# A state-space recurrence put into source order on three engines, with part of the next stages' work set between its groups

## The chip, the cores and the metric

The kernel runs on one core of one Trainium2 chip. The metric is the device time of one launch in microseconds (us). The kernel before takes 2572.84 us, the median of three runs (2568.23 to 2574.86). Everything else about time in this document is read from one profiled execution.

## The reference

The input is `x` (512 tokens x 512 channels) and a context of 8192 x 512. Three blocks follow each other, all in f32, and each adds its result to its input:

```python
x = x + cross_attention(layernorm(x), ctx)       # 16 heads of 64, 8192 keys
u = layernorm(x)
x = x + mamba_and_mlp(u)
x = x + experts(layernorm(x))

def mamba_and_mlp(u):
    h = rmsnorm(u) * norm1_w
    xin, z = split(h @ in_proj.T)                 # 1024 channels each
    xin = silu(causal_conv4(xin) + conv_b)
    dt, B, C = split(xin @ x_proj.T)              # 32, 16, 16
    delta = softplus(dt @ dt_proj.T + dt_b)
    # per channel c and state n, over the tokens t, one after the other:
    #   H[t] = exp(delta[t]*A[c,n]) * H[t-1] + delta[t]*xin[t]*B[t,n]
    #   y[t] = sum_n H[t]*C[t,n]
    y = (y + xin * D) * silu(z)
    u = u + y @ out_proj.T
    h = rmsnorm(u) * norm2_w
    return u + (silu(h @ w1.T) * (h @ w3.T)) @ w2.T       # w1, w3: 512 -> 2048

def experts(v):
    # top 2 of 16 experts by v @ router.T, gate sigmoid(logit), 512 -> 512 -> 512 (SwiGLU)
    return gated_sum_of_two_experts(v) + shared_swiglu(v)   # shared: 512 -> 1024 -> 512
```

The recurrence has 1024 channels x 16 states x 512 tokens. It is sequential over the tokens only.

## The kernel before

The first part, the cross-attention, isn't touched. It ends at about 1868 us of the span. All that follows is in `tail`. There the 512 tokens are worked in two halves of 256 (`s` = 0, 1; `H` = 256). Products of weights use f16 pairs (a high and a low part, three matmuls), and their results are scaled by `IW` on the way out of PSUM.

**The steps of a half, by name.**
- `wo_proj(s)` (L1067) is the attention's output projection. It adds to `x_sb`, two 128-token rows at a time.
- `prep(s)` (L774) makes the two norms (`stats`, `rsqrt`), the scaled `h`, its transposes `hT`, the input projection `pxz`, the convolution (on TensorE by diagonal matrices `dg` for half 1), the silu pair `xin` and `xs` (`silu_split`), and the product `psd` that gives dt, B and C. B and C go to DRAM (`bc_d`) and come back broadcast to all 128 partitions by `load_bc(s, k)` (L866), four loads of 128 x 1024 for each of B (k = 0) and C (k = 1), issued on SP.
- `delta(s, q)` (L876) makes delta and `du` (delta times xin) for 256 channels (`q`, two blocks `b` of 128), with five activations on ScalarE and four VectorE steps, then the product `pz` and its silu `zs`. `lnexp` reloads the activation table after each Silu.
- `scan(s, b)` (L906) is the recurrence of one 128-channel block, in four groups of four states. A group has: four exponentials `dA` on ScalarE (L916); in half 1 a copy of the carried state `carry` into column 0 of `hs` (L918); the multiply of B by `du` (L919); the scan itself over 128 x 1028 (L923); in half 0 the copy of the last state out to `carry` (L925); the multiply by C in place (L926); and four identity matmuls that sum the states into the PSUM tile `py` (L929). A block ends with the term of D (L930). There are 64 groups. `dAs` and `hss` hold three buffers each.
- `gate(s, q, yT)` (L932) multiplies `py` by `zs` and splits the product into an f16 pair `yT`.
- `outproj(s, yT, h2)` (L939) is the output projection, the rmsnorm of its sum (`rsqrt` with the tag c) and the transposes into `h2`.
- The MLP of a half has eight blocks of 256 hidden channels. Each block loads three weight tiles, forms `pg` and `pu`, takes `g = silu(pg) * pu`, splits it into the pair `gg` (a ScalarE copy, then a VectorE subtraction), and adds a down product into two accumulators. `ffn` (L963) states the steps plainly; `ffn_ordered` (L989) holds the down product of a block back until the next block's `pg` and `pu` are issued. The shared experts use the same function with four blocks (`RS`).
- `ln2(s, xT)` (L1034) is the last norm (`rsqrt` with the tag d), its transposes and the router's logits `lg`.
- `route()` (L1171) forms the two chosen experts of each token, one-hot rows `oh`, the rank of each token in its expert's list by the matmul `prk`, from it the slot `sg` and the gate `gs`, and scatters all tokens' rows (`xf`) twice into `xd_d` in DRAM by indirect DMAs on POOL's queue. The experts (`moe_load`, `moe_in` and so on) load 128 rows of `xd_d` each; the first of these loads stand on POOL's queue too, behind the scatters.
- `early()` loads, converts and splits one of the first 20 pieces of the experts' weights (`wef` to `we`).

**Shared buffers.** All weight tiles of the projections and the MLP come by `wload` (L766) on SP's queue into five buffers `wpm`, so a load starts when the buffer's last reader is done. `bank_j` gives three PSUM banks in turn for all short products; `acc` gives the longer accumulators.

**What sets the order.** In the recurrence the program states the steps block by block and the Tile scheduler orders the instructions of all engines by its own priorities: a loop over the eight pairs (s, q) calls `scan(s, 2*q)`, one step of `prep(1)` or of the MLP `ffn(0)`, the gate of the pair before, `delta` of the pair after, and `scan(s, 2*q + 1)`. Of the MLP of half 0 seven of the eight blocks are stated there. From `outproj(1)` on TensorE, VectorE and ScalarE keep the source's order (`tc.manual_schedule`); SP and POOL stay with the scheduler. The stages behind it are driven by generators: `ffn_ordered(1)` with `ln2(0)` at its steps 0, 5, 7 and 9, then the four shared blocks of half 0 with `ln2(1)` and the head of `route`, then the four of half 1 with the rest of `route`, then the experts.

The code of both parts follows.

Of the kernel before, what the change touches and what calls it, by code (L numbers as in the profile page):

```python
# [17 lines left out]
P = 128  # L18
# [18 lines left out]
XR = 2 * DM + 4  # L37
NWE = 20
# [601 lines left out]
def tail(tc, a, out, const, scr, ident, x_sb, mlp_d, oT, sum_d, xd_d, psums):  # L640
# [133 lines left out]
    def prep(s):  # L774
# [4 lines left out]
        nc.vector.tensor_scalar(v1, mv[:, :, 1], 1e-5, None, ALU.add)  # L779
        rsqrt(r1, v1, 2, f"a{s}")  # L780
        nc.vector.tensor_mul(v2, r1, r1)
        nc.vector.tensor_mul(v2, v2, mv[:, :, 1])
        nc.vector.tensor_scalar(v2, v2, 1e-6, None, ALU.add)
        rsqrt(r2, v2, 2, f"b{s}")
        nc.vector.tensor_mul(r2, r2, r1)
# [10 lines left out]
        hT[s] = hp  # L796
        transposeT(h, hp[:, 0], hp[:, 1], scale=nw[:, 0])
# [12 lines left out]
        for i in range(4):  # L810
# [4 lines left out]
            xp = m2.tile([P, 2, H + 3], F32, name="xp", bufs=2)  # L815
            nc.scalar.activation(xp[:, :, 3:], ps, AF.Copy, scale=IW)
# [3 lines left out]
            if s:  # L820
                pc = bank_j([P, 2, H], F32, "pc")
                for j in range(2):
                    e = 2 * i + j
                    dg = m2.tile([P, 4, P], F32, name="dg", tag="w2k", bufs=5)
                    for q in range(4):
                        nc.scalar.activation(dg[:, q], ident, AF.Copy, scale=cw[:, e, q : q + 1])
                    for q in range(4):
                        nc.tensor.matmul(
                            pc[:, j, :], lhsT=dg[:, q], rhs=xp[:, j, q : q + H], start=q == 0, stop=q == 3
                        )  # L830
                silu_split(s, i, pc)
# [20 lines left out]
        for i in range(8):  # L852
            nc.tensor.matmul(psd, lhsT=xpw[:, 0, i], rhs=xs[:, 0, i], start=i == 0, stop=False)
            nc.tensor.matmul(psd, lhsT=xpw[:, 0, i], rhs=xs[:, 1, i], start=False, stop=False)
            nc.tensor.matmul(psd, lhsT=xpw[:, 1, i], rhs=xs[:, 0, i], start=False, stop=i == 7)
        xd = m2.tile([64, H], F32, name="xd", tag="w2k", bufs=5)
# [6 lines left out]
        load_bc(s, 0, m1)  # L863
# [12 lines left out]
    def delta(s, q):  # L876
# [6 lines left out]
        rl = w2("rl")  # L883
        nc.scalar.activation(ex, pd, AF.Abs, scale=IW)
# [3 lines left out]
        nc.scalar.activation(lg, u1, AF.Ln)  # L888
        nc.vector.scalar_tensor_tensor(ex, u1, -1.0, ex, ALU.add, ALU.subtract)
# [7 lines left out]
        for j in range(2):  # L897
            mm_block(pz[:, j, :], wz, j, hT[s][:, 0], hT[s][:, 1])
        zs = m2.tile([P, 2, H], F32, name="zs", bufs=2)
        nc.scalar.activation(zs, pz, AF.Silu, scale=IW)  # L900
        lnexp()
        dlu[s, q] = [dl, du, zs]

    turn = [0]

    def scan(s, b):  # L906
        q, j = b // 2, b % 2
        if j == 0:
            dlu[s, q].append(ps_s.tile([P, 2, H], F32, name="py", tag="pss"))
        dl, du, zs, py = dlu[s, q]  # L910
        for nq in range(4):
            dA, hs = dAs[turn[0] % 3], hss[turn[0] % 3]
            turn[0] += 1
            for n in range(4):
                k = nq * 4 + n
                nc.scalar.activation(dA[:, n, 1:], dl[:, j], AF.Exp, scale=Av[:, b, k : k + 1])  # L916
            if s:
                nc.scalar.copy(hs[:, :, 0], carry[:, b, nq * 4 : nq * 4 + 4])  # L918
            nc.vector.tensor_tensor(  # L919
                hs[:, :, 1:], BC[s][0, nq], du[:, j].unsqueeze(1).to_broadcast((P, 4, H)), ALU.mult  # L920
            )
            hf = hs.rearrange("p n t -> p (n t)")
            nc.vector.tensor_tensor_scan(hf, dA.rearrange("p n t -> p (n t)"), hf, 0.0, ALU.mult, ALU.add)  # L923
            if s == 0:
                nc.scalar.copy(carry[:, b, nq * 4 : nq * 4 + 4], hs[:, :, H])  # L925
            nc.vector.tensor_mul(hs[:, :, 1:], hs[:, :, 1:], BC[s][1, nq])  # L926
            for n in range(4):
                k = nq * 4 + n
                nc.tensor.matmul(py[:, j, :], lhsT=ident, rhs=hs[:, n, 1:], start=k == 0, stop=False)  # L929
        nc.tensor.matmul(py[:, j, :], lhsT=dD[:, b], rhs=xin[s][:, b, :], start=False, stop=True)  # L930

    def gate(s, q, yT):  # L932
        dl, du, zs, py = dlu.pop((s, q))
        y = m2.tile([P, 2, H], F32, name="y", tag="w2k", bufs=5)
        nc.vector.tensor_mul(y, py, zs)
        nc.scalar.copy(yT[:, 0, 2 * q : 2 * q + 2, :], y)
        nc.vector.tensor_tensor(yT[:, 1, 2 * q : 2 * q + 2, :], y, yT[:, 0, 2 * q : 2 * q + 2, :], ALU.subtract)

    def outproj(s, yT, h2, fill=None):  # L939
        wout = [wload("outp", i) for i in range(4)]  # L940
        for i in range(2):
            px = bank_j([P, DM], F32, "px")
            for k in range(8):
                sl = slice(i * P, (i + 1) * P)
                mm_down(px, yT[:, 0, k, sl], yT[:, 1, k, sl], wout[k // 2], k % 2, k == 0, k == 7)
            nc.vector.scalar_tensor_tensor(u_sb[:, 2 * s + i], px, IW, u_sb[:, 2 * s + i], ALU.mult, ALU.add)
        ts_ = slice(2 * s, 2 * s + 2)
# [4 lines left out]
        nc.vector.tensor_scalar(ms, ms, 1e-6, None, ALU.add)  # L952
        rsqrt(rr, ms, 2, f"c{s}")
        h = F.tile([P, 2, DM], F32, name="h", tag="h", bufs=1)
        for i in range(2):
            nc.vector.tensor_scalar(h[:, i], u_sb[:, 2 * s + i], rr[:, i : i + 1], None, ALU.mult)
        if not s:
            nc.vector.tensor_add(x_sb[:, ts_, :], x_sb[:, ts_, :], u_sb[:, ts_, :])
        if fill:
            fill()  # L960
        transposeT(h, h2[:, 0], h2[:, 1], scale=nw[:, 1])

    def ffn(s, h2, names, pm):  # L963
        nf = len(mlp_d[names[0]])
        for f2 in range(nf):
            wg, wu, wd = (wload(n, f2) for n in names)
            pg = bank_j([P, 2, H], F32, "pg")
            pu = bank_j([P, 2, H], F32, "pu")
            for j in range(2):
                mm_block(pg[:, j, :], wg, j, h2[:, 0], h2[:, 1])  # L970
            for j in range(2):
                mm_block(pu[:, j, :], wu, j, h2[:, 0], h2[:, 1])
            g = F2.tile([P, 2, H], F32, name="g32", bufs=2)
            nc.scalar.activation(g, pg, AF.Silu, scale=IW)
            nc.vector.scalar_tensor_tensor(g, pu, IW, g, ALU.mult, ALU.mult)
            gg = F2.tile([P, 2, 2, H], F16, name="gg", bufs=2)
            nc.scalar.copy(gg[:, 0], g)
            nc.vector.tensor_tensor(gg[:, 1], g, gg[:, 0], ALU.subtract)
            yield
            for i in range(2):  # L980
                sl = slice(i * P, (i + 1) * P)
                for j in range(2):
                    k = 2 * f2 + j
                    mm_down(pm[i], gg[:, 0, j, sl], gg[:, 1, j, sl], wd, j, k == 0, k == 2 * nf - 1)
        for i in range(2):
            nc.vector.scalar_tensor_tensor(x_sb[:, 2 * s + i], pm[i], IW, x_sb[:, 2 * s + i], ALU.mult, ALU.add)
# [508 lines left out]
```

## Time and profile before

| what | value |
|---|---|
| median of three runs | 2572.84 us (2568.23 to 2574.86) |
| profiled execution, its own time | 2565.43 us |
| its span on the core | 2563.7 us |
| mean granted TensorE clock | 0.979 of full speed |
| TensorE (PE) busy | 2361.3 us, 92% of the span |
| VectorE (DVE) busy | 2046.2 us, 80% |
| ScalarE (ACT) busy | 1947.5 us, 76% |
| GpSimd (POOL) busy | 73.8 us, 3% |
| moved by DMA | 529.52 MB, 207 GB/s |

The shares are means over stages with different limits, and three quarters of the span are the attention, which the change does not touch. So they say little about the change: it has to be read from the stages behind 1868 us, each by itself. In the profile PE is a matmul, PEld the load of its stationary operand, which runs beside it; SP only issues DMAs. An entry such as `hs<-bc,du` names what is written and what is read, `x64` how often, and a bracket or a last column names the engine, operation and line that ended a wait. L919 is line 919 of the kernel. A stage between two cuts `A:B` is given with its length and with the busy time of each engine in it.

### The profile page before, as it was taken

To read this page: it belongs to the slowest core of one execution; us is meant where nothing else is said; L and a number is where in the kernel's file an instruction comes from. 1 tells how busy PE (TensorE), PEld (TensorE's weight loads), DVE (VectorE), ACT (ScalarE), POOL (GpSimd) and SP (SyncE) were. 2 spreads that over 40 slices of the span, in tenths; PEclk is the share of its full clock that TensorE was granted. 3 is DMA by queue.
4 is the path that set the end of the run, shared out by engine and by line. 5 is a ranking of instruction groups with operands and counts; after the bars stand their busy time and mean duration, and the time that the engine had idled before them with its cause. 6 is when DMAs were issued, how large, how long until landed. Compare 5 with 4: busy or idle time off the path is not lost. (4 is left out here: it accounts for less than half of the span.)

```text
span 2563.7 us, 56681 instructions
## 1 busy us (share of the span) xinstructions
PE 2361.3 (92%) x22958; PEld 1722.3 (67%) x22958; DVE 2046.2 (80%) x2378; ACT 1947.5 (76%) x3734; POOL 73.8 (3%) x77
## 2 busy tenths in 40 slices
PE   7999899999999999999999998998878678899896
PEld 3555577777666777766777776897756456577775
DVE  6776578888888888887888777998899999746685
ACT  5787788888878888877888888997958557434685
POOL 3000000000000000000000000000000000001112
PEclk9999999999999999999999999999999889999998
DMA  7983777787777787777778664777711212388897
GB/s 267 304 272 133 215 213 227 231 238 232 216 231 227 219 247 236 226 213 213 240 216 234 175 171 133 196 207 210 200 59 40 101 50 84 125 281 274 315 360 232
DMA packets 355199, 529.52 MB, mean 207 GB/s; under 512 B 28194, under 2 KB 221922, under 8 KB 354660
## 3 DMA queue, kind: packets, MB, share of 16 engines
q1 hardware_dynamic: 349156, 513.23, 65.7%
q0 software_dynamic: 3616, 8.66, 1.5%
q8 instruction: 182, 2.98, 0.5%
q10 hardware_dynamic: 2160, 3.95, 0.5%
q14 instruction: 85, 0.70, 0.1%
HBM read 396.65 MB, written 126.97 MB: 204 GB/s over the span
## 5 line engine op out<-in xcount | busy, mean ns | idle before, releaser
L380 DVE TENSOR_TENSOR phl<-p,phl 128x1024 f16<-128x1024 f32 x512 | 626.8, 1225 | 191.5 <-ACT phl L377 175.6
L375 ACT ACTIVATE p<-pss 128x512 f32<-128x512 f32 x1024 | 597.6, 622 | 112.1 <-issue 43.5
L308 ACT ACTIVATE sf<-psx 128x512 f16<-128x512 f32 x1024 | 558.6, 625 | 70.2 <-PE psx L303 69.5
L367 PE MATMUL pss<-qhh,k 128*128 128x256 f16 x2048 | 478.3, 274 | 14.1 <-ACT phl L377 11.9
L368 PE MATMUL pss<-qlm,kb 128*128 128x256 f16 x2048 | 477.1, 273 | 0.8 <-DMA v<-v_d 0.7
L316 DVE TENSOR_TENSOR runm<-runm,sf 128x2048 f16<-128x2048 f16 x240 | 292.4, 1220 | 51.4 <-ACT sf L308 51.3
L397 PE MATMUL po<-v,phl 128*128 128x130 f16 x4096 | 322.3, 220 | 3.9 <-DVE oq L410 3.4
L377 ACT ACTIVATE phl<-pss 128x512 f16<-128x512 f32 x512 | 312.8, 611 | 0.0
L397 PEld LDWEIGHTS <-phl 128*128 128x128 f16 x4096 | 270.5, 98 | 61.7 <-issue 15.3
L278 PE MATMUL psv<-wh_v,ctxc 128*128 128x256 f16 x1024 | 283.4, 277 | 7.3 <-ACT wh_v L179 3.2
L279 PE MATMUL psv<-wl_v,ctxc 128*128 128x256 f16 x1024 | 282.0, 275 | 1.1 <-DVE wl_v L180 1.1
L280 PE MATMUL psv<-wh_v,ctxc 128*128 128x256 f16 x1024 | 282.0, 275 | 0.0
L367 PEld LDWEIGHTS <-k 128*128 128x128 f16 x2048 | 200.3, 98 | 65.0 <-issue 20.0
L368 PEld LDWEIGHTS <-kb 128*128 128x128 f16 x2048 | 200.7, 98 | 52.1 <-issue 14.9
L303 PE MATMUL psx<-khl,qh 64*128 64x512 f16 x1024 | 208.1, 386 | 18.2 <-ACT sf L308 13.1
L929 PE MATMUL py<-hs,ident 128*128 128x256 f32 x512 | 141.2, 430 | 76.6 <-DVE hs L926 76.5
L400 PE MATMUL po<-v,phl 128*128 128x65 f16 x4096 | 208.2, 193 | 1.4 <-DVE phl L380 1.4
L254 PE MATMUL psk<-ctxc,wh_k 128*128 128x512 f16 x512 | 197.4, 386 | 10.8 <-ACT ctxc L237 9.0
L379 DVE CAST phl<-p 128x1024 f16<-128x1024 f32 x256 | 176.1, 688 | 30.8 <-ACT p L375 30.6
L255 PE MATMUL psk<-ctxc,wh_k 128*128 128x512 f16 x512 | 196.0, 383 | 0.9 <-DVE ctxc L238 0.9
L256 PE MATMUL psk<-ctxc,wl_k 128*128 128x512 f16 x512 | 195.9, 383 | 0.0
L929 PEld LDWEIGHTS py<-hs,ident 128*128 128x128 f32 x512 | 104.8, 213 | 108.3 <-DVE hs L926 90.9
(315 smaller groups left out, 3814.4 us busy)
## 6 DMA issues: line engine op xcount, KB each, us to landing
v<-v_d SPq DMA_DIRECT2D x128, 520.0 KB
k<-k_d SPq DMA_DIRECT2D x256, 256.0 KB
ctxc<-ctx_d SPq DMA_DIRECT2D x96, 512.0 KB
wef<-in_gu_dram SPq DMA_DIRECT2D x72, 512.0 KB
v_d<-vs SPq DMA_DIRECT2D x128, 260.0 KB
k_d<-khl SPq DMA_DIRECT2D x128, 256.0 KB
kb<-k_d SPq DMA_DIRECT2D x128, 256.0 KB
wpm<-w_d SPq DMA_DIRECT2D x48, 512.0 KB
```

What stands on the lines that cost most here:

```text
L278: nc.tensor.matmul(ps[:, t, :], lhsT=ct[i // 2][:, 0, i % 2, sl], rhs=wh[:, i, :], start=i == 0, stop=False)
L279: nc.tensor.matmul(ps[:, t, :], lhsT=ct[i // 2][:, 0, i % 2, sl], rhs=wl[:, i, :], start=False, stop=False)
L280: nc.tensor.matmul(ps[:, t, :], lhsT=ct[i // 2][:, 1, i % 2, sl], rhs=wh[:, i, :], start=False, stop=i == NC4 - 1)
L308: nc.scalar.activation(dst, ps, AF.Copy, scale=1.0 / (8.0 * WS))
L316: nc.vector.tensor_tensor(r, r, sf, ALU.max)
L367: nc.tensor.matmul(ps[:, hh], lhsT=k[:, hh, sl], rhs=qhh[:, hh, qs], start=True, stop=False)
L368: nc.tensor.matmul(ps[:, hh], lhsT=b[:, hh, sl], rhs=qlm[:, hh, qs], start=False, stop=True)
L375: nc.scalar.activation(p32[:, i], pss[i], AF.Exp, scale=sc)
L377: nc.scalar.activation(ph[:, i], pss[i], AF.Exp, scale=sc)
L380: nc.vector.tensor_tensor(pl, p32, ph, ALU.subtract)
L397: nc.tensor.matmul(o, lhsT=ph[:, i, hh, qs], rhs=vv, start=first, stop=False, **kw)
L929: nc.tensor.matmul(py[:, j, :], lhsT=ident, rhs=hs[:, n, 1:], start=k == 0, stop=False)
```

## The change

The loop over (s, q) and `scan` are replaced by a loop over the 64 groups, one slot per group, and the manual order now opens ahead of this loop: TensorE, VectorE and ScalarE keep the source's order through the recurrence too. In slot g stand, in this order: the carries, the exponentials of group g+1, the multiply and the scan of group g, the multiply by C of group g-1, and the sums of group g-2; then, in fixed slots of each eight, the two steps of a gate and four steps of a `delta`; then side work. The side work of half 0 (slots 0 to 31) is `wo_proj(1)` and `prep(1)`. That of half 1 (slots 36 to 63) is `outproj(0)`, the whole MLP of half 0, its `ln2` and two of the four blocks of its shared experts. `PACE` says how many of its steps a slot takes (1.3 and 1.4). The generators have more `yield` marks, so that the two ends of a hand-off between engines can lie in two slots. `ffn` is gone; `ffn_ordered` can do a range of blocks. The broadcast loads of B and C for half 1 stand at slots 31 and 32. Behind the recurrence, `ffn_ordered(1)` runs without `ln2(0)`, half 0 has two shared blocks left, and `ln2(1)` stands at their steps 3, 5 and 7, with `route` from step 8 on.

```diff
+PACE = (1.3, 1.4)
...
@@ prep(s): more marks, only for half 1
         nc.vector.tensor_scalar(v1, mv[:, :, 1], 1e-5, None, ALU.add)
+        if s:
+            yield
         rsqrt(r1, v1, 2, f"a{s}")
+        if s:
+            yield
...
+                yield
+                pc = bank_j([P, 2, H], F32, "pc")
...
+                yield
                 silu_split(s, i, pc)
...
-        load_bc(s, 0, m1)
+        if not s:
+            load_bc(s, 0, m1)
...
@@ delta(s, q)
         rl = w2("rl")
+        yield
         nc.scalar.activation(ex, pd, AF.Abs, scale=IW)
...
         nc.scalar.activation(lg, u1, AF.Ln)
+        yield
         nc.vector.scalar_tensor_tensor(ex, u1, -1.0, ex, ALU.add, ALU.subtract)
...
+        dlu[s, q] = [dl, du]
+        yield
         zs = m2.tile([P, 2, H], F32, name="zs", bufs=2)
         nc.scalar.activation(zs, pz, AF.Silu, scale=IW)
         lnexp()
-        dlu[s, q] = [dl, du, zs]
-    turn = [0]
-    def scan(s, b):
...
+        dlu[s, q].append(zs)
+        yield
+    def exps(g):
+        s, b, nq = groups[g]
+        dA = dAs[g % 3]
+        for n in range(4):
+            k = nq * 4 + n
+            nc.scalar.activation(dA[:, n, 1:], dlu[s, b // 2][0][:, b % 2], AF.Exp, scale=Av[:, b, k : k + 1])
+    def states(g):
...
+        nc.vector.tensor_tensor(
+            hs[:, :, 1:], BC[s][0, nq], du[:, b % 2].unsqueeze(1).to_broadcast((P, 4, H)), ALU.mult
+        )
+        hf = hs.rearrange("p n t -> p (n t)")
+        nc.vector.tensor_tensor_scan(hf, dA.rearrange("p n t -> p (n t)"), hf, 0.0, ALU.mult, ALU.add)
+    def carry_in(g):
...
+            nc.scalar.copy(hss[g % 3][:, :, 0], carry[:, b, nq * 4 : nq * 4 + 4])
+    def carry_out(g):
...
+            nc.scalar.copy(carry[:, b, nq * 4 : nq * 4 + 4], hss[g % 3][:, :, H])
+    def outputs(g):
...
+        nc.vector.tensor_mul(hs[:, :, 1:], hs[:, :, 1:], BC[s][1, nq])
+    def sums(g):
...
+        for n in range(4):
+            nc.tensor.matmul(py[:, j, :], lhsT=ident, rhs=hs[:, n, 1:], start=nq + n == 0, stop=False)
+        if nq == 3:
+            nc.tensor.matmul(py[:, j, :], lhsT=dD[:, b], rhs=xin[s][:, b, :], start=False, stop=True)
...
@@ outproj(s, yT, h2)
                 mm_down(px, yT[:, 0, k, sl], yT[:, 1, k, sl], wout[k // 2], k % 2, k == 0, k == 7)
+                if k % 4 == 3:
+                    yield
...
+        yield
         rsqrt(rr, ms, 2, f"c{s}")
+        yield
...
-        if not s:
-            nc.vector.tensor_add(x_sb[:, ts_, :], x_sb[:, ts_, :], u_sb[:, ts_, :])
-        if fill:
-            fill()
+        nc.vector.tensor_add(x_sb[:, ts_, :], x_sb[:, ts_, :], u_sb[:, ts_, :])
+        yield
         transposeT(h, h2[:, 0], h2[:, 1], scale=nw[:, 1])
-    def ffn(s, h2, names, pm):
...
-    def ffn_ordered(s, h2, names, pm):
+    def ffn_ordered(s, h2, names, pm, lo=0, hi=None):
...
-        for f2 in range(nf):
+        for f2 in range(lo, hi or nf):
...
@@ the recurrence; taken out is the loop over (s, q) with scan, gate, delta, outproj(0) and ffn(0)
+    groups = [(s, b, nq) for s in range(2) for b in range(8) for nq in range(4)]
+    def side0():
+        yield from wo_proj(1)
+        xin[1] = const.tile([P, 2, 8, H], F32, name="xin1", tag="big16")[:, 0]
+        yield from prep(1)
+    def side1():
+        yield from outproj(0, yTs[0], h2s[0])
+        yield from ffn_ordered(0, h2s[0], MLP, [acc(3), acc(3)])
+        xT0 = h2tile()
+        yield from ln2(0, xT0)
+        rs0.extend([xT0, [acc(3), acc(3)]])
+        yield from ffn_ordered(0, xT0, RS, rs0[1], 0, 2)
...
+    exps(0)
+    for g in range(64):
+        s, b, nq = groups[g]
+        i, r = g // 8, g % 8
+        carry_in(g)
+        if g:
+            carry_out(g - 1)
+        if g + 1 < 64:
+            exps(g + 1)
+        states(g)
+        if g:
+            outputs(g - 1)
+        if g == 31:
+            for _ in sides[0]:
+                pass
+            load_bc(1, 0, m1)
+        if g == 32:
+            load_bc(1, 1, m3)
+        if g > 1:
+            sums(g - 2)
+        if r == 2 and i:
+            gt_ = gate(*seq[i - 1], yTs[-1])
+            next(gt_)
+        if r == 3 and i:
+            next(gt_)
...
+            dl_ = delta(*seq[i + 1])
+        if r in (3, 4, 5, 6) and i < 7:
+            next(dl_)
+        if s == 0 or g > 35:
+            due += PACE[s]
+            while given < due:
+                given += 1
+                next(sides[s], None)
+    outputs(63)
+    sums(62)
+    sums(63)
...
+    for n, _ in enumerate(outproj(1, yTs[-1], h2s[1])):
+        if n >= 4:
+            next(sides[1], None)
+    for _ in sides[1]:
         pass
...
@@ behind the recurrence
-    xT0, xT1 = h2tile(), None
-    l0 = ln2(0, xT0)
     for n, _ in enumerate(mlp1):
-        if n in (0, 5, 7, 9):
-            next(l0, None)
         if n % 3 == 1:
             early()
...
-    for n, _ in enumerate(rs0):
-        if n in (4, 5, 7):
+    for _ in ffn_ordered(0, rs0[0], RS, rs0[1], 2, 4):
+        n += 1
+        if n in (3, 5, 7):
             next(l1, None)
         elif n > 7:
             next(ro, None)
         if n % 3 == 1:
             early()
+    for _ in l1:
+        pass
```

## The prediction, made before the changed kernel ran

> **What bounds the kernel now.** I read the stage table first (busy time of each engine between cuts that I set at the first `hs` multiply, at the end of the last `hs*C` multiply, at the start of the second half's MLP, at its end, at the start of half 1's shared experts and at the start of the experts).
>
> ```profile
> core 0: us, PE busy (x) PEld busy (x) DVE busy (x) ACT busy (x) POOL busy (x), PEclk, DMA share, GB/s
> 1868.32:2217.66 349.34, 264.85 (x1385) 198.15 (x1384) 337.04 (x299) 222.88 (x498) 4.68 (x5) 0.92 0.21 68
> 2217.66:2246.60 28.94, 28.19 (x173) 17.85 (x172) 10.38 (x24) 8.79 (x14) 0.14 (x1) 1.00 0.62 213
> 2246.60:2312.61 66.01, 64.62 (x513) 48.30 (x512) 28.35 (x43) 24.85 (x35) 0.00 (x0) 1.00 0.81 276
> 2312.61:2347.40 34.79, 33.72 (x287) 25.14 (x286) 21.85 (x46) 17.87 (x24) 0.00 (x0) 1.00 0.77 266
> 2347.40:2381.06 33.66, 31.48 (x246) 23.39 (x243) 20.80 (x43) 11.63 (x15) 12.92 (x14) 1.00 0.89 316
> 2381.06:2563.70 182.64, 155.16 (x2088) 127.11 (x2088) 125.74 (x123) 131.04 (x159) 33.12 (x18) 0.95 0.88 298
> ```
>
> The reader is to see that two stages have different owners. In the recurrence (349.3 us) VectorE works 337.0 us and idles 12.3: it is the bound. In the next four rows TensorE works 158.0 of 163.4 us. The change takes TensorE work out of these rows and puts it into the first, where TensorE has room, but with it VectorE work, where VectorE has none. Then the groups of VectorE in the recurrence, and its order of time:
>
> ```profile
> L923 DVE TENSOR_TENSOR_SCAN hs<-dA,hs 128x1028 f32<-128x1028 f32 x64 | 145.3, 2291 | 2.6 <-ACT dA L916 2.5
> L926 DVE TENSOR_TENSOR hs<-hs,bc 128x1024 f32<-128x1024 f32 x64 | 76.9, 1216 | 1.1 <-ACT carry L925 1.1
> L919 DVE TENSOR_TENSOR hs<-bc,du 128x1024 f32<-128x1024 f32 x64 | 76.0, 1216 | 0.7 <-PE py L929 0.6
> ```
>
> ```profile
> 1937.72 1.20 DVE L919 TENSOR_TENSOR hs<-bc,du 128x1024 f32<-128x1024 f32 x1
> 1938.84 1.22 DVE L926 TENSOR_TENSOR hs<-hs,bc 128x1024 f32<-128x1024 f32 x1
> 1939.97 2.29 DVE L923 TENSOR_TENSOR_SCAN hs<-dA,hs 128x1028 f32<-128x1028 f32 x1
> ...
> 1946.64 1.20 DVE L919 TENSOR_TENSOR hs<-bc,du 128x1024 f32<-128x1024 f32 x1
> 1947.88 2.30 DVE L923 TENSOR_TENSOR_SCAN hs<-dA,hs 128x1028 f32<-128x1028 f32 x1
> ```
>
> From start to start a multiply takes 1.12 to 1.13 us when the next instruction is another group's (1937.72 to 1938.84), 1.24 when the next is its own scan (1946.64 to 1947.88). The groups lose only 4.4 us to others: the scheduler has put other work into every wait. What an unfilled wait costs shows after the recurrence, where the order is already that of the source:
>
> ```profile
> 2239.09 0.16 DVE L672 TENSOR_TENSOR nw_c<-rr 128x2 f32<-128x2 f32 x1 [1.78 <-ACT rr L670]
> ...
> 2257.28 0.69 DVE L1015 SCALAR_TENSOR_TENSOR g<-pu,g 128x512 f32<-128x512 f32 x1
> 2258.65 0.69 DVE L1018 TENSOR_TENSOR gg<-g,gg 128x512 f16<-128x512 f32 x1 [0.68 <-ACT gg L1017]
> ```
>
> Last, what TensorE waits for at the start of the experts, and POOL's order of time there:
>
> ```profile
> PE pxd L1315 <- DMA xd<-xd_d: 2.2, 1, 2.2
> ```
>
> ```profile
> 2351.84 1.11 POOL L1238 COPY xf<-gs 128x4 f32<-128x4 f32 x1 [130.89 <-DVE gs L1236]
> ...
> 2363.60 0.41 POOL L1238 COPY xf<-gs 128x4 f32<-128x4 f32 x1 [5.21 <-DMA xd_d<-xf,sg]
> ...
> 2377.71 1.68 POOL L1300 DMA_DIRECT2D xd<-xd_d  x3 [7.56 <-DMA xd_d<-xf,sg]
> ```
>
> From the router's result `gs` (2351.8) to the first expert's transposes (2381.06) there are 29.2 us of two scatters in a row and a load, all on POOL's queue. Today it is 2.2 us later than the shared experts' end. That is the second bound, hidden so far.
>
> **The change part by part.** By the built order nothing is added or dropped on TensorE, VectorE, POOL and SP; ScalarE has three more table loads. All of it is order.
>
> *VectorE in the recurrence.* It starts from the same place (the same attention work precedes it).
> - Today's idle time goes: -12.3.
> - Moved in: two more g/gg pairs (4 x 0.60 = 2.4), the two adds of the MLP into `x_sb` (1.2), ln2's statistics, small steps and two scalings (3.7), its two low-half subtractions (1.2): +8.5.
> - 64 scans now stand directly behind their own multiply (two do today): 62 x 0.12 = +7.4. Here a rule speaks otherwise. The Trainium skill, page VectorE: DVE Perf Modes, section "The DRAIN you can't avoid", has a chain with a semaphore after each instruction take as long as one without; by it this term is 0. The trace's two starts differ by 0.12, and I take the trace.
> - Chains that were interleaved and now stand alone: 21 steps of `delta` 0.12 dearer, a dozen 128x2 steps 0.20 rather than 0.10 apart: +3.7.
> - New waits. The first scan waits for its exponentials, which ended at 1871.9 as before, with nothing to fill it: 2.4. Eight `gg` directly behind their `g` while ScalarE copies: 1.37 rather than 0.60, 8 x 0.77 = 6.2. Three rsqrt (b of norm 1, c, d) with both ends in one slot: 1.78 + 1.78, and for d one table load of 1.28 more, 3.1: 6.7 (that of a is split over two slots). `xs` in the slot where `delta`'s five activations (3.0) stand before the four silus on ScalarE: 2.0. Sum +17.3.
>
> So 349.3 - 12.3 + 8.5 + 7.4 + 3.7 + 17.3 = 373.9, or +24.6.
>
> *ScalarE* has per slot 2.0 (four exponentials and a carry) and side work; in the second half 4.9 us against VectorE's 6.0, in the first 4.0 against 5.3. It runs ahead, so I cost its reloads at nothing (three more, 3 x 1.28, with 126 us free). `carry_in(g)` stands behind the side work of slot g-1, and the scan waits for it: cover is about 1.8 us. If it is gone, see the second rival.
>
> *TensorE* in slots 36 to 63: sums 28 x 0.95, output projection 10.4, eight MLP blocks of 7.83 (48 x 0.109 + 24/2 x 0.216), half a shared block, z and delta, some 113 us of 28 x 5.2 = 146 us. It fits; a `sums(g-3)` has a slot's slack before the multiply that waits for its buffer.
>
> *SP and POOL.* The loads of two shared blocks and the last of the MLP (3 MB and more) move into a stage where DMA is busy 0.21; cost 0. The eight broadcast loads of B and C for half 1 stand on SP in front of the MLP's weights, behind one weight load that waits for a z product of slot 29; each has three or more slots (14 us) to land. POOL is not passed until the scatters.
>
> *Behind the recurrence.* I go through the four rows.
> - 28.9 becomes 27.3. The last sums are one group (1.1), not two; `pu` 2.6, projection 10.4, one block and a down half 7.8; then the transposes wait for the norm's chain (22.2), 1.7, and the last down half, delayed by its `gg`, 3.4.
> - 66.0 becomes 64.0: ln2's transposes (0.9) and logits (0.6) of half 0 are gone, and one `gg` wait.
> - 34.8 becomes 21.3: two shared blocks (15.7) leave, but ln2 of half 1 now has `pg`, `pu` (5.2) in front of its transposes and needs 8.7 from the MLP's end (7.4 today, 1.28 for a table load): 3.5 of wait. 15.7 + 1.5 + 0.6 + 3.5.
> - 33.7 becomes 45.7. Today the rank product `prk` stands in front of half 1's shared experts and `gs` is ready 4.4 us into them. In the new order `prk` stands behind three of their pieces (7.9), and on VectorE the chain is: `x_sb` 0.9, `xf` 2.2, maxima 1.6, `ef` and `we` 1.4, `oh` 0.65, `we` 1.15, g/gg 2.0, two `we` 2.6, then 3.8 from `rk` to `gs`: 16.3. POOL's 29.2 follow, with 0.2 to reach it. TensorE has 31.3 us of work and then waits 14.
>
> Sum 158.3 for 163.4: -5.1. Without the scatter chain it would be 145, or -18.4. That idle brings a second rule against the change: TensorE: Matmul & The Clock Gate, Part 1, has the clock fall to half after some 3.4 us of idling and stay so for about as long once busy, which would cost 1.7 us. The trace has this already: after today's wait the experts' first matmuls take 0.43 us for four (2383.6) and 0.22 from 2385.8. So 0. Experts' stage: unchanged (its 20 weight pieces are ready in both).
>
> Eight of the 20 pieces now load beside half 1's shared experts (six today): 20 x 0.524 MB in 31.3 us is 335 GB/s, against 357 seen in the experts. I take 0; up to +3.
>
> Sum: +24.6 - 5.1 = +19.5. The profiled execution took 2565.4 (span 2563.7), which gives 2585; the median of the three runs is 2572.8, 7.4 above it, and on that scale I say **2592**.
>
> **Rivals.**
> 1. *VectorE does not wait.* ScalarE and TensorE run a slot ahead, so each `gg`, `nw` and `xs` finds its operand. For it: ScalarE is busy 222.9 of 349.3. Against: `g` and `gg` are neighbours on VectorE, and the copy between them can't start before `g` ends. Recurrence 349.3 - 12.3 + 8.5 + 7.4 + 3.7 + 2.4 = 359.0, +9.7, and -5.1: 2577, not slower by what can be told. It decides if the 14.9 us of hand-off waits shrink below 3.
> 2. *ScalarE holds the scans.* A silu or copy that waits for TensorE or VectorE stands in front of the carries and exponentials of the next slot. Its waits today reach 2.1 us for `g` and 5.2 for the norm. 8 to 10 blocks at 2.1 more: +17 to +21, 2609 to 2613. For it: one order for three engines. Against: the slack above.
> 3. *The scatter chain does not bind*: `gs` is early after all, or its 29.2 us shrink with fewer loads in flight. Then -18.4: 2579. With half of rival 1 it is faster, some 2565 or less.
>
> That the change does not do what it says I exclude: in the built order 39 of the 45 pieces stand before the last slot's end.
>
> **How the numbers follow.** My case 0.62, own range 2581 to 2604 (recurrence +16 to +32, chain +-4). Rival 1 0.12, rival 2 0.12, rival 3 0.14. About 0.3% (7.7 us) is what a measurement of this kernel can tell from no change. Slower by more: my case, rival 2, and the upper thirds of 1 and 3: 0.80. Within: 0.12. Faster: 0.08, where 1 and 3 meet. Range 2570 to 2614.
>
> **What would show it.** Right: VectorE's first multiply to last `hs*C` takes 366 to 382; every `g` to `gg` there is 1.37 apart; `nw_b`, `nw_c`, `nw_d` wait 1.8 to 3.1; scan starts 1.24 after its multiply; TensorE waits 10 to 16 for `xd<-xd_d`; `gs` comes 14 to 19 after the start of half 1's shared experts. Wrong: a recurrence under 362, or scans that wait for `carry` or `dA` more than 10 us in all, or TensorE's wait for `xd` under 5.

## The result, and the profile after

The changed kernel takes 2598.52 us (median of four runs, 2591.04 to 2601.07); the kernel before took 2573.56 beside it. The ratio is 1.0096, with a 95% interval of 1.0071 to 1.0121: slower by about 25 us. The forecast was 2592, slower, in a range of 2570 to 2614.

The stage table of the changed kernel, cut at the same events as before (busy time of each engine, then the granted clock, the share of the DMA engines and GB/s):

```profile
core 0: us, PE busy (x) PEld busy (x) DVE busy (x) ACT busy (x) POOL busy (x), PEclk, DMA share, GB/s
1871.58:2256.70 385.12, 290.81 (x1541) 218.00 (x1540) 353.98 (x318) 234.93 (x515) 1.26 (x5) 0.89 0.23 70
2256.70:2284.51 27.81, 27.55 (x167) 17.32 (x166) 11.35 (x26) 8.30 (x13) 0.14 (x1) 1.00 0.64 220
2284.51:2347.15 62.64, 62.64 (x481) 46.94 (x480) 21.45 (x27) 19.60 (x27) 0.00 (x0) 1.00 0.85 290
2347.15:2369.04 21.89, 19.57 (x153) 13.96 (x152) 13.36 (x23) 12.06 (x16) 0.00 (x0) 0.92 0.67 229
2369.04:2412.23 43.19, 31.91 (x255) 23.63 (x253) 26.02 (x61) 15.03 (x19) 14.77 (x14) 0.91 0.84 284
2412.23:2597.20 184.97, 155.71 (x2088) 127.80 (x2088) 125.76 (x123) 131.14 (x159) 31.19 (x18) 0.94 0.87 291
```

The recurrence grew from 349.3 to 385.1 us. The four rows behind it shrank from 163.4 to 155.5, with a TensorE that is idle for 11.3 of the last one's 43.2. The spans differ by 33.5: +35.8 in the recurrence, -7.9 behind it, +2.3 in the experts and +3.3 before the recurrence starts, where the instructions are the same (over all runs below that start lies between 1868.2 and 1875.0, so it is scatter). The medians differ by 25, since the profiled execution of before lies 8 below its median (2565.4 against 2573.6).

The groups of VectorE in the recurrence (count, busy time, mean ns, idle time before them and who ended it):

```profile
L945 DVE TENSOR_TENSOR_SCAN hs<-dA,hs 128x1028 f32<-128x1028 f32 x64 | 147.2, 2300 | 11.1 <-ACT hs L950 2.9 <-ACT dA L935 2.4
L941 DVE TENSOR_TENSOR hs<-bc,du 128x1024 f32<-128x1024 f32 x64 | 78.0, 1218 | 0.0
L960 DVE TENSOR_TENSOR hs<-hs,bc 128x1024 f32<-128x1024 f32 x64 | 76.7, 1200 | 0.0
L1040 DVE TENSOR_TENSOR gg<-g,gg 128x512 f16<-128x512 f32 x8 | 5.5, 692 | 6.4 <-ACT gg L1039 6.4
L819 DVE TENSOR_TENSOR xs<-xin,xs 128x512 f16<-128x512 f32 x4 | 2.8, 691 | 5.2 <-ACT xs L817 5.2
```

One instruction takes as long as before. VectorE as a whole is idle for 31.1 us rather than 12.3 and busy for 354.0 rather than 337.0. Of these 17.0 more busy us some 8.3 are moved work (e_auto below has the same instructions in 345.3); the rest is overlap that is gone: an instruction recorded with 1.20 us can be followed by an unrelated one 1.12 after its start, so that the two records overlap, and the neighbours of the changed kernel do this less often. Of the scan's 11.1 us of idle time only 5.3 have another engine as releaser; the rest is the short gap behind its own multiply, at the 61 other scans, as the order of time shows (start, duration):

```profile
1928.50 1.22 DVE L941 TENSOR_TENSOR hs<-bc,du 128x1024 f32<-128x1024 f32 x1
1929.75 2.30 DVE L945 TENSOR_TENSOR_SCAN hs<-dA,hs 128x1028 f32<-128x1028 f32 x1
1931.96 1.20 DVE L960 TENSOR_TENSOR hs<-hs,bc 128x1024 f32<-128x1024 f32 x1
1933.08 1.22 DVE L941 TENSOR_TENSOR hs<-bc,du 128x1024 f32<-128x1024 f32 x1
1934.40 2.30 DVE L945 TENSOR_TENSOR_SCAN hs<-dA,hs 128x1028 f32<-128x1028 f32 x1
```

A multiply runs 1.25 us to its own scan at 1928.50, 1.32 at 1933.08, and a multiply by C 1.12 to the next multiply (1931.96). The longer case is the common one. At the other end, TensorE's wait at the start of the experts, and on POOL the first and second preparation of the scatters and the loads of their rows:

```profile
PE pxd L1380 <- DMA xd<-xd_d: 11.3, 1, 11.3
```

```profile
2385.10 1.11 POOL L1306 COPY xf<-gs 128x4 f32<-128x4 f32 x1 [125.08 <-DVE gs L1304]
...
2396.78 0.19 POOL L1306 COPY xf<-gs 128x4 f32<-128x4 f32 x1 [3.36 <-DMA xd_d<-xf,sg]
...
2409.11 1.68 POOL L1365 DMA_DIRECT2D xd<-xd_d  x3 [5.48 <-DMA xd_d<-xf,sg]
```

From `gs` to the experts 27.1 us pass (29.2 before), and `gs` now comes 16.0 us into half 1's shared experts, not 4.4.

### The profile page after: what moved, and what is told of

The parts are those of the page before. It is cut to its first block, busy times and chain, and to the rows that moved or that the text cites. A ratio compares the mean times of both kernels' runs of the same rounds, so it can differ in the third digit from the quotient of the medians.

```text
span 2597.2 us, 56698 instructions
## 1 busy us (share of the span) xinstructions
PE 2376.0 (91%) x22958; PEld 1733.0 (67%) x22958; DVE 2055.3 (79%) x2378; ACT 1950.8 (75%) x3737; POOL 71.7 (3%) x77
## 5 line engine op out<-in xcount | busy, mean ns | idle before, releaser
L376 ACT ACTIVATE p<-pss 128x512 f32<-128x512 f32 x1024 | 599.1, 624 | 112.5 <-issue 43.4
L971 PE MATMUL py<-hs,ident 128*128 128x256 f32 x512 | 151.9, 448 | 88.0 <-DVE hs L960 87.9
```

Of the source, the lines that this page charges most:

```text
L376: nc.scalar.activation(p32[:, i], pss[i], AF.Exp, scale=sc)
```

## The experiments

The theory after the result: VectorE is the bound of the recurrence; in source order its hand-offs (to itself, and through ScalarE) lie bare, where the scheduler had other work in them; and what TensorE wins behind the recurrence is taken by the scatter chain. Rivals: the content (the moved work collides with the recurrence in any order), TensorE, ScalarE's queue, and weight loads instead of the chain.

Recurrence is from the first multiply to the end of the last multiply by C, "behind" from there to the first transposes of the experts, both of the profiled execution; the ratio is to runs of the kernel before on the same chip, so two kernels are compared by their ratios rather than by their medians. The recurrence of e_route has the changed kernel's instructions in the same order on the three engines, and took 3.2 us longer (388.3): of a single trace some 3 us in this column are scatter.

| kernel | median us | ratio (95%) | recurrence | behind | wait for xd |
|---|---|---|---|---|---|
| before | 2573.6 | 1 | 349.3 | 163.4 | 2.2 |
| changed | 2598.5 | 1.0096 (1.0071 to 1.0121) | 385.1 | 155.5 | 11.3 |
| e_auto | 2572.1 | 1.0004 (0.9996 to 1.0013) | 356.0 | 158.6 | 11.5 |
| e_swap | 2583.9 | 1.0051 (1.0035 to 1.0068) | 372.6 | 153.9 | 10.3 |
| e_gg | 2596.4 | 1.0102 (1.0084 to 1.0121) | 384.2 | 155.5 | 11.7 |
| e_nosum | 2596.4, one run | | 385.3 | 153.5 | 11.1 |
| e_gg_pool | 2593.2 | 1.0082 (1.0068 to 1.0095) | 378.2 | 153.5 | 11.0 |
| e_late2 | 2584.0 | 1.0043 (1.0029 to 1.0057) | 371.1 | 157.4 | 0 |
| e_late3 | 2576.2 | 1.0013 (1.0002 to 1.0024) | 362.2 | 158.3 | 0 |
| e_pace | 2608.5 | 1.0140 (1.0124 to 1.0155) | 374.0 | 173.8 | 9.9 |
| e_route | 2596.8 | 1.0107 (1.0086 to 1.0128) | 388.3 | 153.5 | 7.9 |
| e_auto2 | 2565.5 | 0.9973 (0.9960 to 0.9985) | 355.3 | 157.0 | 0 |
| e_auto3 | 2560.1 | 0.9961 (0.9947 to 0.9975) | 356.0 | 150.3 | 0 |
| e_ctrl | 2566.7 | 0.9984 (0.9976 to 0.9993) | 348.6 | 161.5 | 0 |

**Order or content (e_auto).** The line that opens the manual order moves from ahead of the loop to behind `outputs(63)`.

> The changed kernel's statements, but the source order of the three engines is imposed only from behind the last group on; through the recurrence the scheduler orders them. It tells the order from the content. Theory (the loss is the order: waits and hand-offs that nothing fills): VectorE idles some 12 us again, the recurrence is 338 + 8.5 of moved work + 12 = 355 to 362 rather than 385, and the whole is 20 to 30 shorter than the changed kernel, about the time of before or a little under. Rival (the content: two more blocks and the norm beside the recurrence collide with it, whatever the order): the recurrence stays above 375.

```profile
1873.14:2229.16 356.02, 282.59 (x1502) 210.32 (x1501) 345.31 (x318) 244.12 (x520) 1.75 (x5) 0.92 0.24 76
```

The same 318 instructions of VectorE take 356.0 us, 29 fewer, and it idles 10.7 of them. So in the recurrence the order costs 29 us and the content 6.7 (356.0 against 349.3). TensorE gets less of its work done beside it, though (1502 matmul records, not 1541), and the row behind the recurrence takes 32.2 us rather than 27.8: over both stages the order costs 26. The whole can't be told from before.

**The own hand-off (e_swap).**

```diff
         hs[:, :, 1:], BC[s][0, nq], ... ALU.mult
     )
+    if g:
+        outputs(g - 1)
     hf = hs.rearrange("p n t -> p (n t)")
     nc.vector.tensor_tensor_scan(hf, ...)
...
         states(g)
-        if g:
-            outputs(g - 1)
```

> In each slot the multiply by C of the group before now stands between the multiply and the scan of a group, so that no scan follows its own multiply. In the changed kernel a multiply takes 1.32 us from its start to that of its own scan (56 of 64 slots) and 1.25 in eight; between unrelated instructions 1.12. Theory (VectorE's hand-offs to itself count): 56 x 0.20 + 8 x 0.13 = 12 us go; the recurrence (385.1) becomes 372 to 376 and the whole is 10 to 12 shorter than the changed kernel. Rival (ScalarE holds the scans): the scans then wait for dA or carry instead, and the recurrence stays above 381. Second rival (a semaphore between neighbours costs nothing, the 0.2 is the scan's own start): no change, 384 to 386.

```profile
1967.87 1.20 DVE L941 TENSOR_TENSOR hs<-bc,du 128x1024 f32<-128x1024 f32 x1
1968.99 1.22 DVE L962 TENSOR_TENSOR hs<-hs,bc 128x1024 f32<-128x1024 f32 x1
1970.12 2.29 DVE L947 TENSOR_TENSOR_SCAN hs<-dA,hs 128x1028 f32<-128x1028 f32 x1
```

All three starts are now 1.12 or 1.13 apart. The recurrence lost 12.6 us, and the ratio fell by 0.45%, some 11.6 us: as the theory says, and the scan has no slow start of its own.

**The bare wait of gg, and what stands behind it (e_gg, e_nosum, e_gg_pool).** In e_gg the subtraction is held back by one slot; nothing else moves:

```diff
-            nc.vector.tensor_tensor(gg[:, 1], g, gg[:, 0], ALU.subtract)
+            later(lambda g=g, gg=gg: nc.vector.tensor_tensor(gg[:, 1], g, gg[:, 0], ALU.subtract))
...
             outputs(g - 1)
+        flush()
```

> Of the blocks beside the recurrence only the subtraction that makes the low half gg is moved: it stands one slot later on VectorE, behind the next group's multiply, scan and multiply by C, not directly behind g. Nothing else moves on any engine. Theory (each gg waits for ScalarE's copy with nothing to fill it): eight waits, 6.4 us together, go, the recurrence falls from 385.1 to 378 to 380. Rival (VectorE would wait elsewhere anyway, for ScalarE or TensorE): the waits return at g, at the scans or at the sums, and the recurrence stays above 383.

This expectation failed: the recurrence fell by 1.0 only. The view of VectorE's waits of e_gg (us in all, times, longest) has no `gg` any more, but

```profile
DVE xs L819 <- ACT xs L817: 6.0, 3, 2.9
DVE hs L945 <- ACT hs L950: 4.9, 4, 2.2
DVE x_sb L1061 <- PE acc L719: 2.7, 2, 1.4
```

2.0 more at the carry and 2.7 new for TensorE's `acc`. The waits at `xs` (6.0 rather than 5.2) and at `pwo` (1.5 rather than 0.9) are longer too, but they lie in half 0, which the edit doesn't touch; slots 32 to 63 alone fell from 201.2 to 198.7. What stands on ScalarE in front of the longest of the four waits for the carry (the scan starts at 2137.16, after 2.17 us of idle time) is not a copy of `gg`:

```profile
2133.21 1.28 ACT L910 ACT_TABLE_LOAD   x1
2134.50 0.63 ACT L910 ACTIVATE lgu<-u 128x512 f32<-128x512 f32 x1
2135.15 1.28 ACT L1046 ACT_TABLE_LOAD   x1
2136.45 0.60 ACT L1046 ACTIVATE g<-pg 128x512 f32<-128x512 f32 x1
2136.94 0.19 ACT L950 COPY hs<-carry 128x4 f32<-128x4 f32 x1
```

In e_nosum three quarters of the sums of half 1 are left out:

```diff
-        for n in range(4):
+        for n in range(1 if s else 4):
```

> The changed kernel with three of the four identity matmuls of each group of half 1 left out, so the recurrence's result for half 1 is not the reference's. VectorE and ScalarE have the same work; TensorE has some 1.4 us less in each of slots 32 to 63. It asks whether TensorE holds the last stretch: slots 48 to 63 took 94.2 us in the changed kernel with VectorE busy 85.7 and TensorE 81.5, and 94.1 with the low halves gg moved. Theory (TensorE and the path over it bind there as much as VectorE): the stretch falls to 86 to 89. Rival (VectorE's own order and its hand-offs to ScalarE hold it alone): it stays at 93 to 95.

From the start of slot 48 to the start of slot 63, first of the changed kernel, then of e_nosum:

```profile
2156.63:2250.84 94.21, 81.52 (x501) 60.62 (x499) 85.67 (x79) 60.98 (x116) 1.26 (x5) 0.91 0.34 104
```

```profile
2155.22:2248.79 93.57, 66.02 (x411) 44.14 (x409) 85.58 (x80) 61.10 (x116) 0.79 (x5) 0.83 0.34 104
```

TensorE has 15.5 us less to do and the stretch is 0.6 shorter. The amount of TensorE's work doesn't hold it, although TensorE is 87% busy there. (The sums were taken out of the changed kernel, not out of e_gg, so the 2.7 us at `acc` are not tested by this.) ScalarE's queue is the next suspect. In e_gg_pool the two copies `carry_in` and `carry_out` of e_gg are `nc.gpsimd.tensor_copy`.

> The changed kernel with the low halves gg one slot later, as in the run that moved them alone, and with the 64 copies of carry made on POOL, which is idle, not on ScalarE. Moving gg alone took its eight waits (6.4 us) away and gave nothing: on ScalarE the copy of the carried state stands behind the copy of gg, and the scan waited for it (2.9 us became 4.9). Theory (ScalarE's one queue holds the scans, as the prediction's second rival has it, once the hand-offs of VectorE go): with the carries off ScalarE the gain of moving gg appears, the waits for carry go, and the recurrence falls from 384.2 to 375 to 379. Rival (the exponentials, which stand behind the same side work, hold the scans just as well, or POOL's copy is too slow): the recurrence stays above 382.

The waits for the carry are gone and the recurrence falls by 6.0, to 378.2; slots 32 to 63 are 6.9 shorter than in the changed kernel. The waits account for this: 6.4 at `gg` and 2.9 at the carry are gone, 2.2 at `acc` are new. So a part of the gain of moving `gg` had been lost to ScalarE's queue. The reason given beforehand, that the carry stood behind the copy of `gg`, does not fit the trace of e_gg: at three of the four scans that wait (4.4 of the 4.9 us) the carry stands behind a table load and the silu of `g`, as in the lines above, and only at one (0.5) behind a copy of `gg`. With VectorE no longer held at `gg`, it reaches the scan before ScalarE is through. The carries on POOL without the move of `gg` were not run, so how the 6.9 us divide between the two edits is read from the waits only.

**All hand-offs one slot later (e_late2, e_late3).** `later` is also put around `xs`, the low halves of `hT` and `h`, and the last four steps of `rsqrt`; `outputs` is placed as in e_swap, and the scatter chain as in e_auto2 (below). e_late3 has the carries on POOL besides.

> Source order throughout, with the multiply by C between multiply and scan, with every VectorE step that needs a ScalarE result of the same side step (low halves gg, xs, hT and h, and the last four steps of each rsqrt) put one slot later, and with the scatter chain as in the run with the scheduler's order. Theory: slots 0 to 31 lose xs, hT, nw (some 9 us) and the own hand-offs, 179 to 184 in the changed kernel to 169 to 172; slots 32 to 63 are held by TensorE in their last third and fall less, the recurrence to 358 to 364; with the shorter chain the whole is 2562 to 2570. Rival (waits come back elsewhere, as with gg alone): recurrence above 369, whole above 2574.

> The run with all hand-offs one slot later and the multiply by C ahead of the scan (recurrence 371.1, of it 11.2 us of waits of the multiply by C for the carry out and 3.7 of the scan for the carry in), with the carries on POOL. Theory (ScalarE's queue holds VectorE): both waits go and the recurrence falls to 356 to 362, the scheduler's 355 to 356; the whole to 2568 to 2575. Rival (exponentials or POOL's latency take their place): recurrence above 367, whole above 2579.

The two largest waits of VectorE in e_late2:

```profile
DVE hs L983 <- ACT carry L978: 11.2, 5, 4.9
DVE hs L968 <- ACT hs L973: 3.7, 4, 1.3
```

and in e_late3:

```profile
DVE hs L962 <- PE py L994: 2.9, 4, 1.0
DVE hs L968 <- ACT dA L956: 2.5, 2, 2.4
```

e_late2 missed: with `outputs` earlier, the multiply by C has to wait until ScalarE has carried the last state out, which stands behind its side work. All 11.2 us of this lie in slots 0 to 31, so that these stayed at 183.5 us (183.9 in the changed kernel), and the other half fell more than expected, from 201.2 to 187.6. With the copies on POOL both waits go, and 371.1 becomes 362.2, 6 to 7 us from the scheduler's order. All of this remainder lies in slots 0 to 31 (175.0 us; 166.9 in e_auto2, which has the same scatter chain); 2.4 of it are the first scan's wait for its exponentials, which the scheduler's order does not have. In slots 32 to 63 the source order is no slower (187.2 against 188.4). The whole came to 2576.2, and both numbers lie just above what was expected: the row behind the recurrence took 35.2 us rather than 27.8. There TensorE waits 2.1 for the norm's `h`, among others, with less work left to put in.

**Less work moved (e_pace).** `PACE = (1.3, 1.15)`.

> The changed kernel with 1.15 side steps for each slot of half 1 rather than 1.4, so that seven steps (half 0's last norm and the shared block) leave the recurrence and stand behind it. Theory (TensorE and the path over it bind in slots 48 to 63): the stretch from slot 36 to 63 falls from 175 to 163 to 167, by more than the 4 us of VectorE work that leave it, and the rows behind grow by 10 to 18 us: the whole within 5 of the changed kernel. Rival (VectorE alone): the stretch falls by 4 to 6 only, and the whole is 8 to 14 longer.

To the start of slot 63, slots 36 to 63 fell from 175.5 to 162.1, more than the first theory expected, but its reason is refuted by e_nosum. VectorE is 7.3 us less busy there, not 4, and the other 6 are shorter waits, above all 2.5 less at the carry, 1.8 at `nw_d` and 1.6 at `gg`. The rows behind grew by 18.3, just above the first theory, and the whole was 0.44% longer, some 11 us, as the rival has it: moving these steps pays even in the poor order.

**The scatter chain (e_route, e_auto2, e_auto3, e_ctrl).** e_route advances the last norm and the router by a few steps.

```diff
-        if n in (3, 5, 7):
+        if n in (3, 4, 5):
             next(l1, None)
-        elif n > 7:
+        elif n > 5:
             next(ro, None)
+        if n == 8:
+            next(ro, None)
```

> Behind the recurrence, the last steps of the second half's norm stand at steps 3, 4 and 5 of the two shared blocks of half 0 rather than 3, 5 and 7, and the router's first four steps at 6 to 8, so that the rank product comes with the first piece of half 1's shared experts, not the third, and the gate gs and the scatters some 7 to 9 us earlier. Theory (the scatter chain of 27 to 29 us on POOL binds): TensorE's wait for xd falls from 11.3 to 2 to 5 us and the whole by 6 to 9. Rival (the weight loads or the DMA rings bind there, not the time of gs): the wait stays at 9 to 12.

It failed: the wait for `xd` fell to 7.9 only, between the two expectations, and the whole did not fall. `gs` was ready 10.0 us into half 1's shared experts rather than 16.0, but the chain took 32.5 us rather than 27.1 (its two waits for landing 5.3 and 8.0 rather than 3.4 and 5.5), and TensorE waited 2.4 for the one-hot rows. The 153.5 us behind the recurrence are no gain: e_nosum and e_gg_pool have the same with the old steps. e_auto2 has e_auto's order in the recurrence and e_route's earlier norm and router, sets the rank product behind the first block's two products, and gives the chain a shorter form:

```diff
+        nc.gpsimd.tensor_copy(xfs[:, 1, :, 0 : XR - 2].bitcast(F32), xf[:, :, 0 : XR - 2].bitcast(F32))
...
-            nc.gpsimd.tensor_copy(xf[:, :, XR - 2 : XR].bitcast(F32), gs[:, :, j : j + 1])
+            nc.gpsimd.tensor_copy(xfs[:, j, :, XR - 2 : XR].bitcast(F32), gs[:, :, j : j + 1])
...
-                    in_=xf[:, i], in_offset=None,
+                    in_=xfs[:, j, i], in_offset=None,
```

> The kernel with the scheduler's order in the recurrence (2572.1), and behind it two changes to the scatter chain: the router's steps earlier, with the rank product behind the first block's two products so that TensorE does not wait for it, and a second copy of the tokens' rows with their other gate (made by POOL ahead of gs), so that the second scatter does not wait for the first to land. The waits for landing in the chain were 5.3 + 8.0 us with the steps earlier. Theory (the chain from gs to xd binds): gs is 5 to 7 earlier and the chain 21 to 24 long rather than 27; TensorE's wait for xd falls from 11.5 to 0 to 3, and the whole to 2560 to 2565, faster than before. Rival (the landing of the scattered rows is set by the weight loads in flight): the chain stays at 27 to 32 and the whole at 2568 to 2572.

The wait for `xd` went from 11.5 to 0, and the whole to 0.9973 of before. From `gs` to the loads of the rows 21.8 us pass on POOL, 24.4 in e_auto. The row, though, shrank by 2.8 only (43.4 to 40.6), because TensorE now waited 3.6 for `g` and 3.3 for a weight tile. By the ratios e_auto2 is some 8 us faster than e_auto; its trace shows only 1.6 of them behind the recurrence and 0.7 in it, and where the others are is open (the experts' stage, 2.0 shorter, is within its scatter). e_auto3 sets the rank chain one step later and loads `early()` at every second step of the MLP, not every third.

> The fastest so far (the scheduler's order in the recurrence, earlier router, two copies of the rows: 2565.5) waited for xd no longer, but TensorE waited 3.6 us for g, which stood behind the whole chain from rk to gs on VectorE, and 3.3 us for a weight tile. Here the rank chain stands one step later, and 13 of the 20 weight pieces are loaded beside half 1's MLP rather than 9. Theory (VectorE's order and the loads hold that row now): both waits shrink to under 3 us together, the row from half 1's shared experts to the experts falls from 40.6 to 35 to 37, and the whole is 3 to 5 shorter, 2560 to 2563. Rival (the loads move the wait into the MLP's row, where DMA is busy 0.85): the MLP's row grows by as much and the whole stays at 2564 to 2568.

The row of half 1's shared experts is the second line here, the MLP of half 1 the first:

```profile
2256.60:2319.20 62.60, 62.60 (x481) 46.96 (x480) 26.71 (x31) 23.49 (x31) 0.00 (x0) 1.00 0.90 322
...
2340.50:2374.51 34.01, 32.22 (x256) 23.53 (x254) 19.95 (x57) 11.34 (x16) 12.87 (x14) 1.00 0.81 283
```

The row of the shared experts takes 34.0 us, 32.2 of them TensorE's, and the MLP's row took the loads for nothing (62.6 as in e_auto2). This is the fastest version: 0.9961 of before. e_ctrl puts only the second copy of the rows and the earlier loads into the kernel before.

> The kernel before, its recurrence and its split of the work untouched, with only what the fastest run changed around the experts' start: a second copy of the rows so that the second scatter does not wait for the first, and 13 of the 20 weight pieces beside half 1's MLP. It asks how much of the 13 us by which that run beats the kernel before comes from these two alone. Theory (they only matter because work was moved away from the scatter chain's cover; here the chain binds by 2.2 us): 1 to 4 faster than before, 2569 to 2572, so that some 9 to 12 of the 13 come from the moved work. Rival (the loads and the chain cost the kernel before as much): 8 or more faster, 2565 or less.

It is 0.16% faster than before (0.07 to 0.24), some 4 us, the upper end of the theory. Of e_auto3's 0.39%, about 0.23% or 6 us are therefore left for the moved work and the router's earlier steps together, less than the 9 to 12 expected; these two were not separated.

## Why the prediction was right, and where its steps were off

The direction, the two bounds and their places held: VectorE owns the recurrence and pays for bare hand-offs, and the scatter chain takes most of what TensorE wins. The size held less well. The sum was +19.5; the trace has +27.9 in these stages. The recurrence grew by 35.8 for the 24.6 forecast, and its 385.1 us lie above the 366 to 382 named as the sign of being right; the rows behind it shrank by 7.9 for 5.1. That the whole came within 7 us of 2592 is in part luck: the terms that were too small were partly made up for by one that was too large (the rsqrt), by the rows behind, and by a profiled execution of before that lies 8 us below its median. Of the other signs the wait for `xd` and the time of `gs` came true; the waits of `nw_b` and `nw_c` (0.5 each) did not, and neither did the start of a scan 1.24 after its multiply (1.32 at most of them).

- **Own multiply to scan:** 7.4 was too small; the group of multiplies takes 10.5 more from start to start, the waits for other engines left out. I took 1.24 from two starts of before. There are two prices: eight scans of the changed kernel wait for VectorE alone and start 1.25 or 1.26 after their multiply; 56 wait for a second engine too, and where that is not late (53) they start 1.31 to 1.34 after it. The rule of the Trainium skill (VectorE: DVE Perf Modes, "The DRAIN you can't avoid") made this term 0, from a chain of eight copies; for a scan behind its own multiply e_swap shows that it is real.
- **Moved work and chains:** 8.5 and 3.7 forecast; about 8.9 and 4.5 in the start-to-start times.
- **New waits:** 17.3 forecast, 23.6 found. The first scan (2.4) and the eight `gg` (6.2, found 6.4) were right; seven of the eight start 1.36 to 1.38 after their `g`, where 1.37 was forecast, and one 2.26. The rsqrt were too dear (6.7; found 2.8): the operand of b and of c is ready a slot earlier, which leaves 0.5 each, and d waits 1.78 without a table load on top. `xs` was too cheap (2.0; found 5.2 in two waits). Not seen at all: the low halves of the transposes (2.2), the carry (2.9) and results of TensorE (1.7).
- **A wait is not its own price.** I added waits as if each could be had back. e_gg took 6.4 us of them away and got 1.0. That sum forecasts the order as it stands, not what removing one term brings.
- **Rival 1** fell: VectorE does wait. **Rival 2** (ScalarE holds the scans) was 2.9 us in the changed kernel, and the next bound as soon as a hand-off was taken out (e_gg, e_late2). I costed it at nothing for its cover of 1.8 us; at two scans a silu (0.6) and its table load (1.28) used that up, at one of them behind the five activations of `delta`. **Rival 3** fell: the chain binds, with 11.3 us of TensorE's wait for the 14 forecast.
- **TensorE** was sized too small in slots 36 to 63, at some 113 us; to the start of slot 63 the trace has it busy for 146.0. A group's sums are eight matmul records 0.22 apart, some 1.7 us, not 0.95. It did no harm, since TensorE did not hold the stretch (e_nosum).
- **Behind the recurrence** the rows were forecast 27.3, 64.0, 21.3, 45.7 and came 27.8, 62.6, 21.9, 43.2; `gs` at 16.3, found 16.0. Without the chain the four rows come to 143.9 by the prediction's own terms (27.3 + 64.0 + 21.3 + 31.3), not to 145; nothing but the third rival's 2579 rests on it.
- **The experts** were costed at no change and came +2.3. Over the other kernels this stage is 181.0 to 186.4 long, so no cause is shown. The matmuls of weights at its start that run at half rate last 3.4 us (from 2414.4 to 2417.7) against 2.5 before, which by my estimate, half of the difference, is some 0.4.

## What to carry to other kernels

When one engine is 97% busy in a stage, moving other engines' work beside it costs about the work it brings to that engine (6.7 us here, for some 8.3 of VectorE work) only as long as the order still fills that engine's waits; writing the order by hand means placing every producer and its consumer a slot apart, on the consumer's queue and on the producer's. Removing a bare wait pays only if the engine behind it can keep up: look for what stands behind the producer in its queue. And a gain behind a stage is worth what the next hidden chain leaves of it, so shorten that chain first (here a second copy of 8 KB a partition, and loads moved to a row that had room).

## What the runs showed of the hardware that was not expected

- A scan directly behind its own multiply on VectorE starts 1.25 us after it, and 1.32 where it also waits for another engine, against 1.12 to 1.14 for an unrelated neighbour. The second price goes with an event-semaphore row in front of the scan: in the changed kernel the 56 scans that have one are those that start at 1.31 or later. Before, 20 scans have such a row:

```profile
L945 DVEq EVENT_SEMAPHORE  x56: 21/21/2281, 1872.8 to 2252.1; - x56
```

```profile
L923 DVEq EVENT_SEMAPHORE  x20: 21/21/2284, 1869.6 to 2211.0; - x20
```

  In e_swap, where 34 scans have such a row but another instruction lies in front of all but one, 61 of 63 scans start 1.13 to 1.14 behind it: then it costs nothing.
- 64 copies of 128 x 4 on POOL did VectorE no harm that could be seen in the recurrence (busy 353.1 us in e_gg_pool, 353.4 in e_gg).
- Scatters that start earlier may land later: in e_route, whose scatters start 6 us earlier in that row, the waits for landing were 13.2 us in all, not 8.8. That the weight loads in flight are the cause was not tested by itself.
